# Four VectorE steps of a fused two-layer model's first layer, moved to ScalarE and to accumulating DMAs

## The chip, the core and the metric

The kernel runs on one NeuronCore of a Trainium2 chip. Five engines work side by side, each with its own instruction queue that is worked through in order: PE (TensorE, matrix products; its weight loads are shown apart as PEld), DVE (VectorE), ACT (ScalarE), POOL (GpSimd) and SP (SyncE, which only starts DMAs here). ACT and POOL can start DMAs too. The metric is the device time of one launch in microseconds (us). The kernel before took 2626.24 us, the median of 3 runs (2625.56 to 2628.49).

## The reference: what is computed

Two layers, each `x + attention(norm(x)) + experts(norm(x))`, for 8 samples of 512 tokens with 256 features, all in float32. Only the attention of layer 0 is touched. For one sample, with `xn` the normalised input:

```python
xc  = conv(xn, conv_w)                 # 3 taps along the tokens, each feature by itself
dx  = xc - xn
xxx = xn + dx * maa_x                  # the first mixed input
t5  = tanh(xxx @ maa_w1)               # from it, five mixing weights w, k, v, r, g
m   = einsum(t5, maa_w2)
xw, xk, xv, xr, xg = xn + dx * (maa_w + m[0]), ...
r, k, v = xr @ Wr, xk @ Wk, xv @ Wv ;  g = silu(xg @ Wg)
w   = time_decay + tanh(xw @ decay_w1) @ decay_w2
y   = forward scan + backward scan of S = exp(-exp(w)) * S + k v, read with r
y   = y * sigmoid(dx @ gate_w + gate_b)
yn  = groupnorm(y) * ln_w + ln_b       # the norm and its affine
x   = x + yn * g @ Wo + experts(xn)    # the residual
```

The experts of layer 0 choose 2 of 8 per token; layer 1 has two attentions (one full, one in a window of 64) and 16 small experts.

## The kernel before

Features lie on the 128 partitions in two halves (`c` = 0, 1), tokens along the free axis; so most steps come as two instructions on 128x512 tiles. `big` and `mix` allocate tiles of both halves, 128x1024.

**Order of the work.** Everything in layer 0 is written as Python generators, and `Turns.turn()` advances each of them to its next `yield` once per turn. What the generators issue in this order is the order of the queues of PE, DVE, ACT and SP (`PINNED`); POOL is not pinned, its order is chosen by the planner of the language. A `yield` between an instruction and its user thus sets how many turns of other work lie between them; it starts nothing by itself. In the scan stage one step of the scans is four turns.

**Stages of layer 0.** The prologue normalises the 8 samples (`norm_and_route`, which also writes `xn` transposed to DRAM as `lines[b]` and scores the experts) and runs `projections(0)` beside it; in this stretch each of its three generators is put into the list of a turn twice, so it advances two yields per turn. The scans begin only when `projections(0)` has set `("scans", 0)`. Then `scans` runs, for each sample, 16 steps of four DVE instructions on 128x1024 (lines 942, 951, 959, 964). Beside it, in the same turns, run the placement of the tokens, the 39 chunks of expert matmuls (`experts`), `projections(b + 1)` while sample b is scanned, and `ending(b, c)`, which is added after the last step of each half. `ending(b, 0)` so runs from the middle of sample b's steps on, `ending(b, 1)` in the first turns of sample b + 1; the last one, `ending(7, 1)`, runs after the scans, in the tail.

**`projections`** has three generators. `inputs` loads `xnT` (line 782, SP), makes `dx` in place (789 the first scale, 791 the two taps), then `xxx` (798), then the t5 matmuls on PE (808) and their tanh on ACT (815). `values` and `decays` wait for `inputs`; they contain `mixed`, in which DVE forms `dx * (maa + m)` from PSUM (770), POOL starts a DMA that adds `xn` to it from `xnT` (774, `accum_op=ALU.add`), and after 4 turns (3 for sample 0) PE reads the sum. `xxx` and all other mixed inputs share a pool of two tiles (`xf`). `xnT` has one buffer.

**`ending`**: y times the sigmoid (991), centering by a matmul (995), square (998), variance by matmuls (1006), square root and reciprocal (1012, 1014), spread and transposed (1017, 1023), then DVE's multiply by the inverse deviation (1026), DVE's affine with `ln_w` and `ln_b` (1027) and POOL's multiply by `g` (1028). After the second half, two rounds of eight output matmuls into the one bank of `ps_e` (1038), each followed by DVE's residual add from PSUM into `x` (1043). `x` was loaded by SP when c was 0 (987), and SP stores it to `after[b]` two turns after the last add (1046). SP's queue also carries all loads of `kv` for the scans (916), 8 for each step, into four buffers.

**Into layer 1.** Its tiles take the memory of layer 0's, and its first ACT and DVE instructions (1186, 1188) come after the last store of `x` from it.

Of the kernel before, what the change touches and what calls it, by code (L numbers as in the profile page):

```python
# [28 lines left out]
AF = mybir.ActivationFunctionType  # L29
ALU = mybir.AluOpType  # L30
# [7 lines left out]
B, T, D = 8, 512, 256  # L38
NC = D // P
# [3 lines left out]
PAD = 2  # L43
# [86 lines left out]
def bc(ap, axis, n):  # L130

    shape = list(ap.shape)
    shape.insert(axis, n)
    return ap.unsqueeze(axis).to_broadcast(shape)


def tokens(x):
    return x.rearrange("(n p) d -> p n d", p=P)
# [33 lines left out]
def two_layers(ctx: ExitStack, tc: tile.TileContext, a: dict, out: bass.AP):  # L172
    nc = tc.nc
    vec_e, act_e, pool_e, pe = nc.vector, nc.scalar, nc.gpsimd, nc.tensor
# [33 lines left out]
    def V(name, c):  # L208
        return vecs[:, VEC[name], c : c + 1]
# [177 lines left out]
    with ExitStack() as l0:  # L387
# [302 lines left out]
        def projections(b):  # L690


            first = b == 0
            made[b] = {}

            def big(tag, bufs=2):
                return rw.tile([P, NC, T], F32, tag=tag, name=f"{tag}_{b}", bufs=bufs)

            def bank(name):
                return ps_rw.tile([P, T], F32, tag="rw", name=f"{name}_{b}")  # L700
# [5 lines left out]
            def mix(name, i, other=False):  # L706

                if other and first:
                    return held(i, [P, NC, T], f"{name}_{b}")
                return rw.tile([P, NC, T], F32, tag="xf", name=f"{name}_{b}", bufs=2)  # L710
# [32 lines left out]
            xnT = rw.tile([P, NC, T + 2 * PAD], F32, tag="xnT", name=f"xnT_{b}")  # L743
            xT = [xnT[:, c, PAD : PAD + T] for c in range(NC)]
            dx = big("dx", 1)
            dxs = [dx[:, c, :] for c in range(NC)]
# [4 lines left out]
            def shifted(c, s):  # L751
                return xnT[:, c, PAD + s : PAD + s + T]
# [26 lines left out]
            def inputs():  # L779
                pool_e.memset(xnT[:, :, 0:PAD], 0.0)  # L780
                pool_e.memset(xnT[:, :, PAD + T :], 0.0)
                nc.sync.dma_start(
                    xnT[:, :, PAD : PAD + T], lines[b].rearrange("(c p) t -> p c t", p=P)
                )
                for _ in range(3):
                    yield
                for c in range(NC):
                    o = dx[:, c, :]
                    vec_e.tensor_scalar(o, xT[c], V("conv1", c), None, ALU.mult)
                    for s, n in ((-1, "conv0"), (1, "conv2")):  # L790
                        vec_e.scalar_tensor_tensor(o, shifted(c, s), V(n, c), o, ALU.mult, ALU.add)
                    yield
                for _ in range(0 if first else 1):
                    yield
                both = mix("xxx", 0)
                xxx = [both[:, c, :] for c in range(NC)]
                for c in range(NC):
                    vec_e.scalar_tensor_tensor(
                        xxx[c], dxs[c], V("maa_x", c), xT[c], ALU.mult, ALU.add
                    )  # L800
                for _ in range(1 if first else 2):
                    yield
                both = ((t5a, 0, 0, P), (t5b, P, 64, 96))
                pss = []
                for _, lo, r0, r1 in both:
                    ps = bank(f"t5{lo}")
                    for c in range(NC):
                        pe.matmul(
                            ps[r0:r1, :], m1w[:, c, lo : lo + r1 - r0], xxx[c],
                            start=c == 0, stop=c == NC - 1,  # L810
                        )
                    pss.append(ps)
                    yield
                for (t5, _, r0, r1), ps in zip(both, pss):
                    act_e.activation(t5, ps[r0:r1, :], AF.Tanh)
                yield
                done.add(("inputs", b))
# [21 lines left out]
            def decays():  # L839
# [66 lines left out]
                made[b]["g"] = g  # L906

            return inputs(), values(), decays()


# [16 lines left out]
        def scans(turns):  # L927
# [4 lines left out]
            for n, (b, c, vg) in enumerate(todo):  # L932
# [33 lines left out]
                def sums(b=b, c=c, vg=vg, kv=kv, y=y, z=z, x=x):  # L966
                    for i in range(NV):

                        r0, at = (vg * NV + i) % 4 * 32, (vg * NV + i) // 4
                        pe.matmul(  # L970
                            y[r0 : r0 + 32, :], C["take"][:, 24 - 8 * at : 56 - 8 * at],
                            kv[:, i, :], start=at == 0, stop=at == 3, skip_group_check=True,
                        )
                    if vg == STEPS - 1:
                        turns.add(ending(b, c, y, z, x))
# [7 lines left out]
        def ending(b, c, y, z, x):  # L983

            sig, g = made[b]["sig"], made[b]["g"]
            if c == 0:
                nc.sync.dma_start(x, tokens(a["x"][b]))


            yg = rw.tile([P, T], F32, tag="gn", name=f"yg{c}_{b}", bufs=2)  # L990
            vec_e.tensor_tensor(yg, sig[:, c, :], y, ALU.mult)
            yield
            yield
            yc = ps_e.tile([P, T], F32, tag="e", name=f"yc{c}_{b}")
            pe.matmul(yc, C["center"], yg, start=True, stop=True)
            yield
            sq = rw.tile([P, T], F32, tag="gn", name=f"sq{c}_{b}", bufs=2)
            act_e.activation(sq, yc, AF.Square)
            zc = z[:, c, :]
            act_e.copy(zc, yc)  # L1000
            yield
            yield

            var = ps_rw.tile([P, NT, 8], F32, tag="rw", name=f"var{c}_{b}")
            for t in range(NT):
                pe.matmul(
                    var[:, t, :], sq[:, t * P : (t + 1) * P], C["mean"][:, :8],
                    start=True, stop=True,
                )
            yield  # L1010
            sd = rw.tile([P, NT, 8], F32, tag="sd", name=f"sd{c}_{b}")
            act_e.activation(sd, var, AF.Sqrt, bias=geps)
            yield
            vec_e.reciprocal(sd, sd)
            yield
            wide = rw.tile([P, NT, HD, 8], F32, tag="gn", name=f"wide{c}_{b}", bufs=2)
            act_e.copy(wide, bc(sd, 2, HD))
            yield
            yield
            rs = ps_rw.tile([P, T], F32, tag="rw", name=f"rs{c}_{b}")  # L1020
            for t in range(NT):
                cols = slice(t * P, (t + 1) * P)
                pe.transpose(rs[:, cols], wide[:, t, :, :].rearrange("p v h -> p (v h)"), ident)
            yield
            yield
            vec_e.tensor_tensor(zc, zc, rs, ALU.mult)
            vec_e.tensor_scalar(zc, zc, V("ln_w", c), V("ln_b", c), ALU.mult, ALU.add)
            pool_e.tensor_tensor(zc, zc, g[:, c, :], ALU.mult)
            yield
            if c + 1 < NC:  # L1030
                return
            made.pop(b)
            yield
            for t in range(0, NT, 2):
                ps = ps_e.tile([P, 2, D], F32, tag="e", name=f"o{t}_{b}")
                for i in range(2):
                    for k in range(NC):
                        pe.matmul(
                            ps[:, i, :], z[:, k, (t + i) * P : (t + i + 1) * P], wmix[:, 4, k, :],
                            start=k == 0, stop=k == NC - 1,  # L1040
                        )
                yield
                vec_e.tensor_tensor(x[:, t : t + 2, :], x[:, t : t + 2, :], ps, ALU.add)
            yield
            yield
            nc.sync.dma_start(tokens(after[b]), x)

        for b in range(B):
# [562 lines left out]
```

## Time and profile before

| | |
|---|---|
| Median of 3 runs | 2626.24 us |
| Profiled execution, its own time | 2629.75 us |
| Its span (first to last instruction) | 2628.0 us |
| Mean granted TensorE clock | 0.931 |
| ACT busy | 934.0 us, 36% |
| POOL busy | 475.5 us, 18% |
| DMA, moved in all | 269.80 MB, mean 103 GB/s |
| First step of the scans starts | 99.1 us |
| Last scan instruction of layer 0 ends | about 1394 us |
| First instructions of layer 1 | about 1438 us |

The page gives busy times over the whole span, which has stages with different limits, so the views by stretch count for more than the shares. "Idle before" and "waited for" tell what ended an engine's idle time, by the semaphores; a short wait can hide behind another. In a group's line, "x14 | 9.7, 737 | 0.0" is 14 instructions, 9.7 us together, 737 ns each in the mean, and no idle time before them.

### The profile page before, as it was taken

To read this page: it belongs to the slowest core of one execution; us is meant where nothing else is said; L and a number is where in the kernel's file an instruction comes from. 1 tells how busy PE (TensorE), PEld (TensorE's weight loads), DVE (VectorE), ACT (ScalarE), POOL (GpSimd) and SP (SyncE) were. 2 spreads that over 40 slices of the span, in tenths; PEclk is the share of its full clock that TensorE was granted. 3 is DMA by queue.
4 is the path that set the end of the run, shared out by engine and by line. 5 is a ranking of instruction groups with operands and counts; after the bars stand their busy time and mean duration, and the time that the engine had idled before them with its cause. 6 is when DMAs were issued, how large, how long until landed. Compare 5 with 4: busy or idle time off the path is not lost. (4 is left out here: it accounts for less than half of the span.)

```text
span 2628.0 us, 32310 instructions
## 1 busy us (share of the span) xinstructions
PE 2318.2 (88%) x11772; PEld 1373.0 (52%) x11772; DVE 2064.8 (79%) x2759; ACT 934.0 (36%) x1731; POOL 475.5 (18%) x408
## 2 busy tenths in 40 slices
PE   6599988889989888999845799999999999999998
PEld 4265555555655555655622445554555555555555
DVE  7799989789899987999986655676767668685566
ACT  1334241242322423223101244444444444445444
POOL 1123232323223322332221110010101010000000
PEclk9789998989989989999965899999999999999999
DMA  6646675556657556665552100010110101000000
GB/s 221 162 110 172 174 204 148 153 149 180 193 162 205 152 147 186 175 169 166 154 155 81 57 25 25 9 45 29 33 33 25 37 21 41 17 21 21 21 1 25
DMA packets 111708, 269.80 MB, mean 103 GB/s; under 512 B 25632, under 2 KB 51008, under 8 KB 106432
## 3 DMA queue, kind: packets, MB, share of 16 engines
q0 software_dynamic: 32048, 136.73, 18.7%
q1 hardware_dynamic: 70528, 113.32, 15.7%
q10 hardware_dynamic: 8976, 17.70, 1.9%
q8 instruction: 95, 1.56, 0.2%
q14 instruction: 61, 0.50, 0.1%
HBM read 215.22 MB, written 31.46 MB: 94 GB/s over the span
## 5 line engine op out<-in xcount | busy, mean ns | idle before, releaser
L670 PE MATMUL y<-wdn,h 128*128 128x256 f32 x936 | 274.8, 431 | 43.8 <-DVE h L639 41.4
L951 DVE TENSOR_TENSOR_SCAN kv<-dqs,kv 128x1024 f32<-128x1024 f32 x128 | 292.0, 2282 | 3.1
L959 DVE TENSOR_TENSOR_SCAN kv<-ds,kv 128x1024 f32<-128x1024 f32 x128 | 292.7, 2287 | 1.6
L670 PEld LDWEIGHTS y<-wdn,h 128*128 128x128 f32 x936 | 177.4, 206 | 163.8 <-issue 86.4
L630 PE MATMUL g<-xsT,wgu 128*128 128x256 f32 x936 | 230.4, 390 | 0.7 <-ACT xsT L616 0.7
L1330 ACT ACTIVATE pt_g<-sc_g 128x512 f32<-128x512 f32 (+1 forms) x384 | 170.9, 532 | 151.3 <-PE sc_g L1322 143.5
L1480 PE MATMUL y<-w,h 128*128 128x256 f32 x768 | 203.5, 403 | 5.6 <-DVE h L1469 4.8
L630 PEld LDWEIGHTS g<-xsT,wgu 128*128 128x128 f32 x936 | 177.3, 194 | 53.8 <-issue 30.7
L1424 PE MATMUL g<-xT,w 128*128 128x512 f32 x384 | 193.8, 627 | 9.7 <-DVE h L1466 4.4
L630 PE MATMUL u<-xsT,wgu 128*128 128x256 f32 x780 | 195.4, 390 | 0.2
L1424 PE MATMUL u<-xT,w 128*128 128x512 f32 x384 | 191.4, 621 | 1.8 <-DVE h L1466 0.9
L630 PEld LDWEIGHTS u<-xsT,wgu 128*128 128x128 f32 x780 | 146.9, 193 | 56.0 <-issue 23.9
L1480 PEld LDWEIGHTS y<-w,h 128*128 128x128 f32 x768 | 139.2, 194 | 62.7 <-issue 35.9
L964 DVE TENSOR_TENSOR kv<-kv,r 128x1024 f32<-128x1024 f32 x128 | 164.5, 1285 | 3.4
L942 DVE TENSOR_TENSOR kv<-kv,k 128x1024 f32<-128x1024 f32 x128 | 155.9, 1218 | 13.3 <-DMA w<-in_w 8.2
L654 ACT ACTIVATE h<-g 128x512 f32<-128x512 f32 (+1 forms) x117 | 61.4, 526 | 277.1 <-PE g L630 252.0
L1330 ACT ACTIVATE pt_l<-sc_l 128x384 f32<-128x384 f32 (+1 forms) x256 | 98.2, 471 | 122.6 <-PE sc_l L1322 82.4
L970 PE MATMUL ys<-kv,cst 128*32 128x512 f32 x512 | 96.3, 668 | 50.9 <-DVE kv L964 50.9
L592 POOL DMA_INDIRECT xs<-normed,whose x78 | 121.3, 1555 | 79.2 <-DVE whose L576 47.3
L1467 DVE TENSOR_TENSOR h<-h,u 128x512 f32<-128x512 f32 x96 | 66.1, 688 | 78.3 <-PE u L1424 74.1
L1338 DVE TENSOR_TENSOR pt_l<-pt_l,cst 128x768 f32<-128x768 f32 (+1 forms) x128 | 108.0, 885 | 17.9 <-ACT pt_l L1330 17.9
L1338 DVE TENSOR_TENSOR pt_g<-pt_g,cst 128x512 f32<-128x512 f32 x128 | 85.1, 686 | 39.1 <-ACT pt_g L1330 38.9
(311 smaller groups left out, 3795.0 us busy)
## 6 DMA issues: line engine op xcount, KB each, us to landing
kv<-vd SPq DMA_DIRECT2D x1024, 64.0 KB
xf<-xnT POOLq DMA_DIRECT2D x40, 512.0 KB, 6.6
cb<-cd SPq DMA_DIRECT2D x128, 128.0 KB
outs<-ys POOLq DMA_DIRECT2D x39, 256.0 KB, 6.3
w<-in_w ACTq DMA_DIRECT2D x12, 384.0 KB
xn<-in_x SPq DMA_DIRECT2D x8, 512.0 KB
xnT<-xT ACTq DMA_DIRECT2D x16, 256.0 KB
normed<-xn SPq DMA_DIRECT2D x8, 512.0 KB
```

Of the source, the lines that this page charges most:

```text
L592: pool_e.indirect_dma_start(out=xs[:, n, :], out_offset=None, in_=normed, in_offset=bass.IndirectOffsetOnAxis(ap=whose[:, at : at + 1], ax ...
L630: pe.matmul(o, w[:, at + c * P : at + (c + 1) * P], xT[:, c, :], start=c == 0, stop=c == NC - 1,)
L670: pe.matmul(y[:, n, :], hs[j // 2][lo:, j % 2, n * P : (n + 1) * P], wd[lo:, j * D : (j + 1) * D], start=j == 0, stop=j == NJ0,)
L942: vec_e.tensor_tensor(kv, kv, bc(kc, 1, NV), ALU.mult)
L951: vec_e.tensor_tensor_scan(out=flat, data0=qc, data1=flat, initial=0.0, op0=ALU.mult, op1=ALU.add)
L959: vec_e.tensor_tensor_scan(out=flat[:, ::-1], data0=dc[:, ::-1], data1=flat[:, ::-1], initial=0.0, op0=ALU.mult, op1=ALU.add,)
L964: vec_e.tensor_tensor(kv, kv, bc(rc, 1, NV), ALU.mult)
L970: pe.matmul(y[r0 : r0 + 32, :], C["take"][:, 24 - 8 * at : 56 - 8 * at], kv[:, i, :], start=at == 0, stop=at == 3, skip_group_check=True,)
L1330: act_e.activation(pt[:, i, :end], scs[i][:, :end], AF.Exp, scale=0.25)
L1338: vec_e.tensor_tensor(pt[:, :, a0 : a0 + m], pt[:, :, a0 : a0 + m], bc(mask[:, :m], 1, 4), ALU.mult,)
L1424: pe.matmul(ps, w[:, k, c * P : (c + 1) * P], xT[:, c, :], start=c == 0, stop=c == NC - 1,)
L1480: pe.matmul(y[:, i, :], hs[k][:, (t + i) * P : (t + i + 1) * P], w1[j - 5 + k][:, 2, :], start=k == 0, stop=k == 5,)
```

## The change

- **dx's first scale.** DVE's multiply of `xn` by `conv1` becomes an ACT multiply for both halves, one turn ahead of DVE's two taps. `inputs` is one turn longer by it.
- **The first mixed input.** DVE's `dx * maa_x + xn` becomes an ACT multiply `dx * maa_x` and one DMA from POOL's queue that adds `xn` out of `xnT`; the t5 matmuls follow 4 turns later (3 for sample 0), in place of 2 (1).
- **The norm's affine.** DVE's multiply and add with `ln_w` and `ln_b` becomes one ACT instruction (Identity with a per-partition scale and bias), one turn after DVE's multiply and one turn ahead of POOL's.
- **The residual.** SP's load of `x` goes. ACT copies the two output banks into `x`, a DMA from POOL's queue adds the layer's input from DRAM to it, and SP's store is issued 8 turns after that DMA.

```diff
@@ inputs
                 for _ in range(3):
                     yield
                 for c in range(NC):
+                    act_e.mul(dx[:, c, :], xT[c], V("conv1", c))
+                yield
+                for c in range(NC):
                     o = dx[:, c, :]
-                    vec_e.tensor_scalar(o, xT[c], V("conv1", c), None, ALU.mult)
                     for s, n in ((-1, "conv0"), (1, "conv2")):
                         vec_e.scalar_tensor_tensor(o, shifted(c, s), V(n, c), o, ALU.mult, ALU.add)
                     yield
...
                 for c in range(NC):
-                    vec_e.scalar_tensor_tensor(
-                        xxx[c], dxs[c], V("maa_x", c), xT[c], ALU.mult, ALU.add
-                    )
-                for _ in range(1 if first else 2):
+                    act_e.mul(xxx[c], dxs[c], V("maa_x", c))
+                pool_e.dma_start(both, xnT[:, :, PAD : PAD + T], accum_op=ALU.add)
+                for _ in range(3 if first else 4):
                     yield
@@ ending
             sig, g = made[b]["sig"], made[b]["g"]
-            if c == 0:
-                nc.sync.dma_start(x, tokens(a["x"][b]))
...
             vec_e.tensor_tensor(zc, zc, rs, ALU.mult)
-            vec_e.tensor_scalar(zc, zc, V("ln_w", c), V("ln_b", c), ALU.mult, ALU.add)
+            yield
+            act_e.activation(zc, zc, AF.Identity, bias=V("ln_b", c), scale=V("ln_w", c))
+            yield
             pool_e.tensor_tensor(zc, zc, g[:, c, :], ALU.mult)
...
                 yield
-                vec_e.tensor_tensor(x[:, t : t + 2, :], x[:, t : t + 2, :], ps, ALU.add)
-            yield
-            yield
+                act_e.copy(x[:, t : t + 2, :], ps)
+            pool_e.dma_start(x, tokens(a["x"][b]), accum_op=ALU.add)
+            for _ in range(8):
+                yield
             nc.sync.dma_start(tokens(after[b]), x)
```

## The prediction

> **What bounds the kernel now.** I read the page, then the busy times by stretch, the waits of PE and DVE, the costliest groups, and the timeline of both ends of layer 0. The page's busy line:
>
> ```profile
> PE 2318.2 (88%) x11772; PEld 1373.0 (52%) x11772; DVE 2064.8 (79%) x2759; ACT 934.0 (36%) x1731; POOL 475.5 (18%) x408
> ```
>
> No engine is the bound throughout. The chain on the page covers only the last 5% of the span (from 2501 us), so for layer 0 I go by stretches: 0 to 99 us is the prologue, 99 to 1397 the scans beside the experts, 1397 to 1438 the tail, then layer 1 with PE at 95%. A sample's scans are 16 steps; I cut them into quarters of four steps (16 turns) at VectorE's first instruction of a step. First quarters of samples 1, 2 and 3, and the second one of sample 3; the columns are the stretch, its length, then busy us (and instructions) of PE, PEld, DVE, ACT, POOL, the granted clock, the DMA share, GB/s:
>
> ```profile
> 278.60:318.90 40.30, 38.11 (x151) 22.67 (x150) 39.21 (x37) 13.98 (x20) 13.98 (x9) 0.93 0.47 150
> ...
> 433.90:482.90 49.00, 39.28 (x145) 23.94 (x146) 40.47 (x39) 14.75 (x21) 9.66 (x7) 0.90 0.43 117
> ...
> 610.20:650.60 40.40, 35.34 (x131) 21.01 (x128) 39.78 (x39) 11.31 (x17) 11.09 (x9) 0.95 0.55 160
> 650.60:692.00 41.40, 41.40 (x161) 26.93 (x159) 33.80 (x28) 7.75 (x13) 13.80 (x11) 0.93 0.73 181
> ```
>
> DVE fills 97 to 98% of the first quarters of samples 1 and 3, but PE has only 2.2 and 5.1 us to spare there. Sample 2's is lock-step: both engines wait, 8 to 10 us each. In second quarters PE is full. The pattern repeats every three samples (4 as 1, 5 as 2, 6 as 3). So a microsecond taken off DVE is worth at most what PE has idle in that quarter. Waits of the scan stage (us, times, longest), PE first, then DVE:
>
> ```profile
> PE t L808 <- DVE xxx L798: 9.9, 4, 3.6
> PE v L729 <- DMA xf<-xnT: 6.1, 3, 2.7
> ```
> ```profile
> DVE xf L770 <- PE m L764: 30.5, 15, 5.7
> ...
> DVE dq L884 <- ACT near L879: 9.4, 7, 2.0
> ```
>
> **The change, part by part.** Removed from DVE within the scan stage, with one ACT row to price the replacement:
>
> ```profile
> L1027 DVE TENSOR_SCALAR z<-z,vecs 128x512 f32<-128x512 f32 x15 | 9.7, 650 | 0.5
> L798 DVE SCALAR_TENSOR_TENSOR xxx<-dx,vecs,xnT 128x512 f32<-128x512 f32 x14 | 9.7, 737 | 0.0
> ...
> L1043 DVE TENSOR_TENSOR x<-x,o 128x512 f32<-128x512 f32 x14 | 9.6, 688 | 10.8 <-PE o L1038 10.6
> ...
> L789 DVE TENSOR_SCALAR dx<-xnT,vecs 128x512 f32<-128x512 f32 x14 | 7.1, 507 | 0.0
> ```
> ```profile
> L861 ACT ACTIVATE d<-w,vecs 128x512 f32<-128x512 f32 x14 | 9.1, 686 | 0.3
> ```
>
> Relief: 9.7 + 9.7 + 9.6 + 7.1 = 36.1 us of DVE, 4.5 us of it in a full first quarter (dx 1.0, xxx 1.5, affine 0.65, residual 1.38), 0.65 in a third quarter (the affine of c = 0). What it is worth, quarter by quarter: sample 0 has inputs only, PE idle 24 us: 2.4. Samples 1 and 4: PE's 2.2 idle each, 4.4. Samples 3 and 6: PE idle 5.1 and 5.8 against 4.5 removed, I take 4 each, 8. Sample 7 has the ending only: 2.0. Samples 2 and 5, lock-step: half of 4.5 each, 4.4. Third quarters: seven at half of 0.65, one in full, 3. Sum 24 us. Bounds: 10 (lock-step everywhere) and 36 (all of it).
>
> Added on ACT: 57 instructions of 0.58 us (plain copies) to 0.69 us (L861, with a per-partition operand), some 37 us. Cover: ACT is busy 28 to 35% of a first quarter. If that cover were gone, the work would simply have changed engines and the relief of 24 be nothing. The Trainium skill speaks against the move (ScalarE: Activation LUTs, Rules for kernel authors: plain multiplies and adds belong on VectorE): by its formula (What ACT_TABLE_LOAD costs) an instruction with one such operand takes 280 + 0.833 x 512 = 707 ns, close to L861, against 507 and 650 on DVE. As a rule for time on the path it would leave the other terms below alone, +25.5; by the rows ACT is off the path and the relief stands. No row shows Identity; the same page (Table sets) says that it is in every set, and the trace has loads at no Copy line. Were there two loads each time, 16 x 2 x 1.28 us (L654's load) is 41 us on ACT, still under its idle time.
>
> Waits added. (1) DVE's first dx instruction (L791) waits for ACT's two multiplies, issued one turn (some 2.5 us) ahead, and the scan instructions are queued behind it. Nearest row: dq waiting for near, 9.4/7 = 1.3 us each, with a longer ACT chain. Bounds 0 and 1.3; I take 0.4, in 7 samples 3 us. (2) PE's t5 matmuls (L808) wait for the accumulate into xxx, with projections and expert matmuls queued behind. ACT's multiplies are issued in turn 7, PE in turn 11: 10 us. Needed: ACT 1.3, POOL's issue 1.34, landing 6.6, together 9.2. The same kind of DMA today:
>
> ```profile
> L774 POOL DMA_DIRECT2D xf<-xnT x40: 1183/1340/1810, 61.5 to 1220.6; - x40
> ...
> DMA to landing us min/median/max: 5.1/6.6/9.8
> ```
>
> xf has the same four turns, and PE waits for it 10 us in all over 21 mixes, up to 4.2 us in one quarter. For xf PE is held to DVE by the matmul just before; for xxx nothing holds it, and today it already runs ahead into xxx (9.9 us). Bounds 0 and 4 each; I take 1.3, in 7 samples 9 us. That is on top of the old wait, which is spent in the relief. (3) POOL gets 16 accumulates (8 xxx, 8 x) of 1.3 us and waits in its queue for ACT; behind it are the weight and row loads, which land 6 to 9 us after issue for a use more than 10 later, and no PE wait on them is shown today: nothing. (4) SP loses x's load (0.42 us) and stores x eight turns (20 us) after the accumulate instead of two turns after DVE's add. Accumulate and issue take 8 to 10 us of the 20, so SP's kv loads behind the store come no later: nothing; were the landing over 20 us, they would starve the next scan. (5) The affine adds two turns ahead of POOL's multiply; the output matmul stays two turns behind it: nothing. (6) DMA: 8 x 512 KB more on 269.8 MB, at 60% share: nothing.
>
> The ends have no cover. Prologue:
>
> ```profile
> 39.86 6.57 PE L808 MATMUL t<-xxx,m1w 128*128 128x512 f32 x8 [5.67 <-DVE xxx L798]
> ...
> 52.18 1.94 PE L764 MATMUL m<-t5a,m2a 32*128 32x512 f32 x4
> ```
>
> PE waits for xxx even now, and all of projections(0) follows. In place of xxx (39 to 40.5 us) the second dx pair falls there, then ACT 1.3, POOL 1.3 and 6.6 to land: 49 to 50. Then the 6.6 us of t5, score and transpose matmuls of the next norms (4 us), copies and tanh on ACT (2.5): the first m at 62 in place of 52. Of those 10 us some 4 come back, since one turn of norm work (score and transposes, expert choice) now lies ahead of the chain: +6, bounds 2 and 10. Tail:
>
> ```profile
> 1432.37 0.69 DVE L1043 TENSOR_TENSOR x<-x,o 128x512 f32<-128x512 f32 x1 [3.59 <-PE o L1038]
> ...
> 1433.09 0.38 SPq L1046 DMA_DIRECT2D after<-x  x1
> ...
> 1437.92 0.88 DVE L1188 TENSOR_SCALAR xg_g<-xT,vecs 128x512 f32<-128x512 f32 x2 [4.86 <-DMA after<-x]
> ```
>
> Layer 1's first work waits for the last store of x. Between add and store comes POOL's accumulate: 6.6 us from issue to landing, plus 0.9 for its wake-up and for an affine that ACT may run behind the copy of cT: +7.5, bounds 5 and 10; PE is full from 1500 on and gives none back. Here the skill would say less: DMA: Bandwidth & Descriptors (Anatomy of one DMA) fits 2.0 us + bytes/436 GB/s, 3.2 us for 512 KB, a tail of about +4 and a sum 3.4 lower. The row is 6.6 and I take it.
>
> Sum: -24 + 3 + 9 + 6 + 7.5 = +1.5 us. It stands against the profiled execution (2629.75 us, its span 2628.0), which is 3.5 us over the median of the runs, 2626.24; I add it to the median: **2628**.
>
> **Rivals.** *Slower: the xxx accumulate lands late.* Place: L808 in the first quarters of samples 1 to 7. For it: PE's lead over DVE there, and an issue-to-landing time of up to 9.8. Against: the four turns nearly cover 9.2. At 4 us each (the xf wait of samples 2 and 5) it costs 28 in place of 9: +20, 2646. It decides above 1.8 us a sample. *Faster: the relief counts almost in full.* For it: DVE at 97% in five of seven first quarters, and PE's wait for xxx there goes. Against: PE has 2 to 5 us to give. With 30 of 36 us, no new wait and ends of 13.5: -16, 2610. *The relief moves nothing:* PE sets each quarter, DVE only waits more. For it: lock-step in samples 2 and 5, PE full in second quarters; against: DVE without a wait in the others. Left are the ends and the new waits at half: 2626 + 13.5 + 6 = 2646, or 2640 without waits; I put 2642.
>
> **How the numbers follow.** Forecast 0.45 (its own range 2619 to 2638), late accumulate 0.25, full relief 0.22, no relief 0.08. About 0.2% (5.3 us) is what a measurement of this kernel can tell: the band is 2621 to 2631.5. Faster: 0.21 of the full relief and 0.06 of the forecast, 0.27. Same: 0.24, nearly all the forecast's. Slower: 0.15 of the forecast, 0.25, 0.08 and rounding, 0.49. The range takes in the centres of the rivals and the nearer part of the bounds: 2607 to 2651; beyond lie 36 us of relief with no wait, and 28 + 9 us of waits with the long ends.
>
> **What would show it.** DVE's busy time down 41 us, ACT's up about as much, with no new table loads; a wait of t (L808 before) for DMA xxx near 1 to 2 us a sample; first quarters 1 to 4 us shorter; scans starting some 6 us later; layer 1's first instruction 7 to 8 us behind the end of the tail's copy work. The prediction is wrong if kv loads or expert weights make an engine wait, if POOL's queue puts an accumulate behind a load that waits for PE, or if first quarters keep their length.

## The result, and the profile after

The changed kernel takes 2659.45 us, the median of 4 runs (2657.73 to 2664.2). The kernel before, run beside it on the same chip, takes 2625.9 (2625.36 to 2628.49). The ratio is 1.0129, 95% interval 1.0111 to 1.0146: **slower by 1.3%, some 34 us**, where 2628 was forecast with a range up to 2651.

The busy times moved the way that was forecast. The page's line for the changed kernel:

```profile
PE 2333.0 (88%) x11772; PEld 1384.7 (52%) x11772; DVE 2027.7 (76%) x2695; ACT 976.6 (37%) x1795; POOL 497.5 (19%) x424
```

DVE has 37.1 us less (41 was forecast), ACT 42.6 more (about 41), POOL 22 more. DVE became freer and the kernel slower, so the page's shares do not hold the answer; the stretches do. I cut both traces at the same events; each column is one profiled execution. "Scan stage" runs from DVE's first multiply of kv by k to 7 us behind the start of the last one, "tail" from there to layer 1's first DVE instruction; the four sums are the quarters of all 8 samples (4 steps each).

| us | before | after | difference |
|---|---|---|---|
| First step of the scans starts | 99.1 | 113.8 | +14.7 |
| Scan stage | 1294.6 | 1306.7 | +12.1 |
| of it first quarters | 360.4 | 316.1 | -44.3 |
| second quarters | 313.2 | 347.0 | +33.8 |
| third quarters | 377.2 | 380.9 | +3.7 |
| fourth quarters | 243.8 | 262.7 | +18.9 |
| Tail | 44.2 | 49.9 | +5.7 |
| Layer 1 | 1190.1 | 1187.8 | -2.3 |
| Span | 2628.0 | 2658.2 | +30.2 |

The first quarters gained more than the 36.1 us that was taken off DVE, and second and fourth quarters lost more than that. These are sample 1's second quarter before the change, then first and second quarters of samples 1, 2 and 3 after it (samples are counted from 0; the columns are stretch, length, busy us and instructions of PE, PEld, DVE, ACT, POOL, granted clock, DMA share, GB/s):

```profile
318.90:357.90 39.00, 38.57 (x162) 25.68 (x161) 34.67 (x30) 6.86 (x13) 12.60 (x10) 1.00 0.83 210
```
```profile
298.00:336.40 38.40, 28.29 (x110) 17.47 (x110) 33.59 (x28) 11.42 (x18) 9.71 (x6) 0.91 0.65 168
336.40:386.70 50.30, 49.23 (x190) 31.65 (x190) 36.39 (x33) 14.90 (x23) 16.48 (x13) 0.97 0.65 171
472.40:508.00 35.60, 29.05 (x126) 18.72 (x125) 34.98 (x29) 12.72 (x20) 7.12 (x6) 1.00 0.76 197
508.00:552.10 44.10, 43.26 (x171) 27.13 (x171) 35.82 (x32) 11.86 (x19) 17.00 (x14) 1.00 0.77 207
632.50:668.10 35.60, 32.24 (x130) 20.44 (x127) 35.13 (x30) 13.89 (x21) 12.13 (x9) 1.00 0.73 195
668.10:710.20 42.10, 39.84 (x154) 25.05 (x154) 34.79 (x30) 8.63 (x16) 13.74 (x12) 0.97 0.77 200
```

Look at the instruction counts of PE. In sample 1's first quarter PE had 151 matmuls and has 110; the second had 162 and has 190. Sample 2's move the same way (145 to 126, and 145 to 171), sample 3's hardly. So the quarters of samples 1 and 2 do not hold the same work any more: the next sample's projections come later, in sample 1 PE stands idle for 10 us of the first quarter, and the second takes 50.3 us in place of 39.0. The waits from 99 to 1450 us (us, times, longest) name what is late there; PE first, then DVE:

```profile
PE g L729 <- DMA xf<-xnT: 24.3, 8, 6.3
PE t L809 <- DMA xxx<-xnT: 13.0, 2, 6.8
```
```profile
DVE kv L943 <- DMA kv<-vd: 41.5, 9, 8.3
DVE h L639 <- PE u L630: 35.9, 19, 6.7
DVE q L871 <- ACT d L863: 23.2, 8, 8.9
DVE sd L1013 <- ACT sd L1011: 21.1, 7, 3.7
```

Before, the same lines were 3.9 (g), 2.7 (kv), 13.0 (h), 0.6 (q) and 5.5 (sd). Only the wait of t is for something that the change put in. The others are of parts that it leaves as they were.

**The ends.** The prologue of the changed kernel, in the timeline:

```profile
39.33 1.45 POOL L801 DMA_DIRECT2D xxx<-xnT  x1 [3.58 <-ACT xxx L800]
46.80 6.31 PE L809 MATMUL t<-xxx,m1w 128*128 128x512 f32 x8 [5.88 <-issue]
...
58.20 1.52 PE L764 MATMUL m<-t5a,m2a 32*128 32x512 f32 x4 [2.28 <-ACT t5a L816]
```

The first m matmul is at 58.20 in place of 52.18, +6.0. The other 8.7 us come between it and the scans. And the tail, where from the accumulate's issue to the store of x there are 7.5 us:

```profile
1459.80 1.43 POOL L1045 DMA_DIRECT2D x<-in_x  x1 [6.21 <-ACT x L1044]
1467.30 0.38 SPq L1048 DMA_DIRECT2D after<-x  x1
...
1470.45 0.88 DVE L1190 TENSOR_SCALAR xg_g<-xT,vecs 128x512 f32<-128x512 f32 x2 [20.52 <-DMA after<-x]
```

### The profile page after: what moved, and what is told of

It is laid out like the page before. It is cut to its first block, busy times and chain, and to the rows that moved or that the text cites. A ratio compares the mean times of both kernels' runs of the same rounds, so it can differ in the third digit from the quotient of the medians.

```text
span 2658.2 us, 32351 instructions
## 1 busy us (share of the span) xinstructions
PE 2333.0 (88%) x11772; PEld 1384.7 (52%) x11772; DVE 2027.7 (76%) x2695; ACT 976.6 (37%) x1795; POOL 497.5 (19%) x424
## 5 line engine op out<-in xcount | busy, mean ns | idle before, releaser
L670 PE MATMUL y<-wdn,h 128*128 128x256 f32 x936 | 268.7, 423 | 34.9 <-DVE h L639 31.9
L943 DVE TENSOR_TENSOR kv<-kv,k 128x1024 f32<-128x1024 f32 x128 | 156.0, 1219 | 48.4 <-DMA kv<-vd 41.5
L971 PE MATMUL ys<-kv,cst 128*32 128x512 f32 x512 | 105.2, 679 | 58.7 <-DVE kv L965 58.6
L654 ACT ACTIVATE h<-g 128x512 f32<-128x512 f32 (+1 forms) x117 | 61.4, 526 | 238.2 <-PE g L630 224.9
L582 POOL DMA_INDIRECT wgu<-in_w_gu,wrow x39 | 68.6, 1759 | 303.1 <-PE u L630 301.1
```

The source lines that it names most:

```text
L670: pe.matmul(y[:, n, :], hs[j // 2][lo:, j % 2, n * P : (n + 1) * P], wd[lo:, j * D : (j + 1) * D], start=j == 0, stop=j == NJ0,)
L943: vec_e.tensor_tensor(kv, kv, bc(kc, 1, NV), ALU.mult)
L971: pe.matmul(y[r0 : r0 + 32, :], C["take"][:, 24 - 8 * at : 56 - 8 * at], kv[:, i, :], start=at == 0, stop=at == 3, skip_group_check=True,)
```

## The experiments

Two theories came from these traces. *Shifted turns*: three turns added to `inputs` move the whole chain of the next sample's projections against everything else that is written turn by turn. *Queues*: what was added to POOL's and SP's queues holds up the kv loads and the accumulates into xf.

### One part at a time

Each kernel is the kernel before with one of the four parts of the change, its turns included.

```diff
# e1: the dx part
+                    act_e.mul(dx[:, c, :], xT[c], V("conv1", c))
+                yield
-                    vec_e.tensor_scalar(o, xT[c], V("conv1", c), None, ALU.mult)
# e2: the xxx part
-                    vec_e.scalar_tensor_tensor(xxx[c], dxs[c], V("maa_x", c), xT[c], ALU.mult, ALU.add)
-                for _ in range(1 if first else 2):
+                    act_e.mul(xxx[c], dxs[c], V("maa_x", c))
+                pool_e.dma_start(both, xnT[:, :, PAD : PAD + T], accum_op=ALU.add)
+                for _ in range(3 if first else 4):
# e3: the affine part; e4: the residual part, both as in the change
```

> The kernel before with one part of the change alone: the first scale of dx goes to ACT, one turn ahead. Theory 'shifted turns' (each turn added to the inputs pushes the next sample's projections out of the first quarter, where PE has gaps, into the second, where it has none): prologue +3 us, the scan stage some 3 us longer in spite of 7.1 us less work on DVE, total +3 to +7 us. Theory 'queues' (the loss comes from kv loads that SP issues late, behind the store of x and the write of vd): prologue +3, scan stage -3 to 0 since nothing is added to SP or POOL; total -1 to +3 us.

> The kernel before with xxx alone moved: ACT's multiply, POOL's accumulate, and the two turns that are added before the t5 matmuls. 'Shifted turns': this is the main part of the loss; prologue +9 us, scan stage +5 to +12 us, with first quarters shorter and second quarters longer; total +14 to +21 us. 'Queues': the prologue's +9 us and a wait of PE for the accumulate; scan stage -5 to +3; total +4 to +12 us.

> The kernel before with the norm's affine alone on ACT, with its two turns. 'Shifted turns': the ending's turns lie behind PE's projections and feed no projection, so the 9.7 us of relief count for something: -6 to 0 us. 'Queues': no DMA is added; likewise -6 to 0 us. If the turns before POOL's multiply delay the output matmul into a full quarter: 0 to +4 us.

> The kernel before with the residual alone moved: ACT copies the matmul's result into x, POOL accumulates the input into x, the store follows eight turns later. Tail +6 us in each theory. 'Shifted turns': the inputs keep their turns, so the scan stage gains 0 to 6 us from 9.6 us of relief; total 0 to +6 us. 'Queues': SP's store, moved to the middle of the second quarter, and POOL's accumulate hold the kv loads up; DVE's wait for kv grows from 3 us to 20 us or more; total +12 to +20 us.

| kernel | ratio to before | 95% interval | in us | scan stage | third quarters |
|---|---|---|---|---|---|
| before | | | | 1294.6 | 377.2 |
| e1, dx | 1.0248 | 1.0228 to 1.0268 | +65 | 1368.8 | 440.0 |
| e2, xxx | 1.0179 | 1.0159 to 1.0200 | +47 | 1340.0 | 373.7 |
| e3, affine | 0.9973 | 0.9963 to 0.9983 | -7 | 1286.7 | 370.4 |
| e4, residual | 1.0034 | 1.0017 to 1.0051 | +9 | 1290.8 | 378.8 |

Both theories missed e1 and e2 by far. The dx part alone, one turn and two ACT instructions a sample, costs nearly twice what the whole change costs, and the four parts add up to +114 us against +34 for all of them together. So no price by part exists, and "first quarters against second quarters" is not the mechanism either: e1 loses most in its third quarters. Nor does the prologue have a price by part: the scans start at 99.9 us in e1 and 98.9 in e2, against 99.1 before, where 3 and 9 us had been expected. The affine gained 7 us, a little over its expectation. The residual alone has its tail (+4.5 us). DVE's wait for kv rises from 2.7 to 21.0 us, but the scan stage is no longer for it, and it is not SP's store that holds these loads up: of the two waits, in samples 2 and 5, the first ends at 513.34 us, and the store is issued at 513.60, behind the loads; ahead of them SP had waited 6.4 and 10.2 us for the next sample's v. The total lies between the two expectations.

### Only the turns

What is left of e1 when its moved work is taken out is one `yield`.

```diff
# e5, on the kernel before
                 for _ in range(3):
                     yield
+                yield
                 for c in range(NC):
                     o = dx[:, c, :]
# e6: the same, and
-                for _ in range(1 if first else 2):
+                for _ in range(3 if first else 4):
```

> The kernel before with nothing moved to another engine: one empty turn is added to the inputs, ahead of the dx work. Theory 'place in the turns': a turn moves the next sample's chain against the ending of the sample in the scans, so PE's dw matmul (which waits for the accumulate into xf) comes to stand ahead of the ys matmuls that DVE's yg instruction waits for. Then this kernel loses what the dx part alone lost, +55 to +75 us, with third quarters at 55 to 60 us in place of 46 to 51. Theory 'moved work' (the loss of the dx part comes from ACT's multiplies and DVE's wait for them): -3 to +6 us.

> The kernel before with nothing moved: the three turns that the change adds to the inputs (one ahead of dx, two ahead of the t5 matmuls), empty. 'Place in the turns': second quarters longer by 2 to 10 us as in the changed kernel, scan stage 15 to 40 us longer, since the relief of DVE is missing; total +18 to +45 us. 'Moved work': the turns only delay the prologue; 0 to +8 us.

With one empty turn: ratio 1.0305 (1.0283 to 1.0328), +80 us, a little more than the 55 to 75 expected; third quarters 437.9. With three: 1.0160 (1.0140 to 1.0181), +42 us. Nothing was moved to another engine in either. **The `yield`s alone cost more than the whole change does**; the moved work gives some of it back. Three waits of e6 from 99 to 1450 us are nearly those of the changed kernel:

```profile
DVE kv L943 <- DMA kv<-vd: 48.5, 13, 9.7
PE g L729 <- DMA xf<-xnT: 23.4, 8, 5.4
DVE sd L1015 <- ACT sd L1013: 21.1, 7, 3.7
```

The waits of h for u (20.1 us) and of q for d (13.2) have grown too, but less than in the changed kernel (35.9 and 23.2). So the late kv loads and the late accumulates into xf are no effect of the added DMAs on POOL and SP, which e6 doesn't have. *Queues*, as a theory of what was added to them, falls as the main cause.

What one turn does is seen around the start of sample 3's third quarter, first in the kernel before, then in e5. A "[...]" is the idle time of the engine just before, and what ended it:

```profile
684.77 2.58 POOL L774 DMA_DIRECT2D xf<-xnT  x2 [2.39 <-DVE xf L770]
...
688.70 3.05 POOL L582 DMA_INDIRECT wdn<-in_w_dn,wrow  x1 [1.35 <-PE y L670]
...
692.00 1.93 PE L847 MATMUL dw<-xf,dw 128*64 128x512 f32 x4
```
```profile
722.20 1.40 DVE L770 SCALAR_TENSOR_TENSOR xf<-m,vecs,dx 128x512 f32<-128x512 f32 x2
...
724.77 1.78 POOL L582 DMA_INDIRECT wdn<-in_w_dn,wrow  x1 [8.02 <-PE y L670]
...
727.31 2.60 POOL L774 DMA_DIRECT2D xf<-xnT  x2
...
736.62 3.64 PE L848 MATMUL dw<-xf,dw 128*64 128x512 f32 x4 [6.74 <-DMA xf<-xnT]
...
740.19 1.20 PE L971 MATMUL ys<-kv,cst 128*32 128x512 f32 x8
...
741.50 0.69 DVE L992 TENSOR_TENSOR yg<-sig,ys 128x512 f32<-128x512 f32 x1 [8.07 <-PE ys L971]
```

Before, POOL issues the two accumulates into xf as soon as DVE has made the first tile, and a gather of expert weights (L582) behind them. In e5 that gather, which waits 8 us for PE's y, stands ahead of them, and they are issued 3.7 us after DVE has finished both tiles. It is so in all seven samples of e5 that follow the first: the first accumulate comes 1.1 to 7.7 us after its tile, 32 us together, behind gathers for the experts that waited for PE; before, it comes after 0.3 us each time. POOL's queue is the one that is not pinned, and one turn in `inputs` was enough to change its order. PE waits at dw for the accumulate, issued 9.3 us ahead. Behind dw in PE's queue stand the ys matmuls, for which DVE's yg waits; and behind yg in DVE's queue stand the scans. One late DMA stops both engines that carry the stage. In the kernel before the same dw starts 7.2 us after its accumulate's issue with no gap, and yg waits 2.5. The waits of yg and dw in e5, 7 samples each:

```profile
DVE yg L992 <- PE ys L971: 50.0, 7, 11.2
PE dw L848 <- DMA xf<-xnT: 48.9, 7, 11.4
DVE sd L1015 <- ACT sd L1013: 43.0, 7, 7.6
```

They were 15.8, 3.6 and 5.5. With three turns instead of one, dw falls behind yg (in the changed kernel 715.0 us for yg, 718.5 for dw in that sample), yg waits 4.2 us in all there (6.0 in e6), the accumulate ahead of dw comes 0.3 us after its tile again, and other neighbours collide.

e10 tests the chain from dw to yg: e5's turn stays, and yg moves two turns down, with the rest of the ending behind it.

```diff
# e10, on e5
+            yield
+            yield
             yg = rw.tile([P, T], F32, tag="gn", name=f"yg{c}_{b}", bufs=2)
```

> The kernel before with the one empty turn in the inputs and two empty turns ahead of the ending's yg instruction. If that one turn costs because DVE's yg waits for ys behind the dw matmul: yg's wait of 50 us in the scan stage falls under 15, third quarters lose 25 to 45 us of their 437.9, total +25 to +55 us against the kernel before. If yg's wait is only where a general shortage of PE shows: the wait goes to another instruction, third quarters stay within 10 us of 437.9, total +68 to +85 us.

Ratio 1.0183 (1.0168 to 1.0198), +48 us: two more empty turns in another place give 32 of the 80 us back. Third quarters 407.7, yg's wait 17.0 (under 15 was expected), while dw's stays at 52.3, as POOL's accumulates stay late. The chain dw, ys, yg is thus a large part of the loss of e5, though not all: DVE's wait of h for u grew to 41 us, and PE has a new wait of 53 us, of rs for DVE's xf. No run puts POOL's order back by itself, so how much of the 80 us is due to it stays open.

e11 goes the other way, with nothing moved: from sample 2 on the next sample's inputs start one turn earlier.

```diff
# e11, on the kernel before; sample 1 is added at the start of sample 0 as before
                 yield
+                if (c, vg) == (NC - 1, STEPS - 1) and b + 2 < B:
+                    turns.add(then(*projections(b + 2)))
                 vec_e.tensor_tensor(kv, kv, bc(rc, 1, NV), ALU.mult)
```

> The kernel before with nothing moved, the next sample's inputs starting one turn earlier from sample 2 on. If the place of the kernel before is only good against the turns behind it, one turn the other way is harmless: -8 to +6 us. If its place is a narrow optimum: +15 to +60 us.

Ratio 1.0105 (1.0089 to 1.0122), +28 us. Of the places tried, that of the kernel before is a narrow optimum: one turn down costs 80 us, three 42, one up 28. So a start that is merely earlier is no gain.

### The place given back

If the place is the cause, the changed kernel is mended by starting the chain as much earlier as it got longer.

```diff
# e7, on the changed kernel; sample 1 is added at the start of sample 0 as before
                 if n + 1 == len(todo):
                     done.add(("spread",))
                 yield
+                if (c, vg) == (NC - 1, STEPS - 1) and b + 2 < B:
+                    turns.add(then(*projections(b + 2)))
```

> The changed kernel, with the next sample's inputs started three turns earlier, from sample 2 on, so that its t5 matmuls and all behind them keep the turns that they had before the change. 'Place in the turns': quarters of samples 1 to 6 return to the lengths before, less the relief; scan stage 10 to 30 us shorter than in the changed kernel's 1306.8; total -4 to +14 us against the kernel before. 'Moved work': the scan stage stays near 1307; total +28 to +36 us.

Ratio 0.9986 (0.9971 to 1.0001). The changed kernel's loss of 34 us is gone, with 4 us to spare, and no ACT instruction, no DMA and no turn was taken out of it. The scan stage is 1274.8, which is 32 us under the changed kernel and **20 us under the kernel before**. First and second quarters of samples 1 and 3:

```profile
301.10:337.80 36.70, 36.09 (x144) 22.21 (x143) 36.27 (x32) 15.81 (x23) 15.15 (x11) 1.00 0.72 193
337.80:379.70 41.90, 40.05 (x167) 26.12 (x165) 33.70 (x29) 8.61 (x16) 15.72 (x11) 1.00 0.88 211
626.20:666.00 39.80, 36.14 (x135) 21.68 (x132) 37.61 (x34) 13.31 (x20) 12.49 (x9) 0.91 0.60 174
666.00:703.60 37.60, 37.55 (x156) 24.82 (x156) 32.72 (x27) 8.90 (x15) 16.85 (x12) 1.00 0.89 209
```

PE's 144 and 167 matmuls in sample 1 are near the 151 and 162 of before: the work is back in its quarters. And PE hardly waits for the new accumulate:

```profile
PE t L809 <- DMA xxx<-xnT: 0.7, 2, 0.3
```

### The ends

```diff
# e8, on the changed kernel: the first sample's dx and xxx, and the last sample's
# residual, in the form of before; for example
+                    if first:
+                        vec_e.scalar_tensor_tensor(xxx[c], dxs[c], V("maa_x", c), xT[c], ALU.mult, ALU.add)
+                    else:
                         act_e.mul(xxx[c], dxs[c], V("maa_x", c))
+                if not first:
                     pool_e.dma_start(both, xnT[:, :, PAD : PAD + T], accum_op=ALU.add)
...
+                if last_b:
+                    vec_e.tensor_tensor(x[:, t : t + 2, :], x[:, t : t + 2, :], ps, ALU.add)
+                else:
                     act_e.copy(x[:, t : t + 2, :], ps)
# e9: e8 and e7 together
# e12, on e9
-                act_e.dma_start(vd.rearrange("(c p) t -> p c t", p=P), v)
+                pool_e.dma_start(vd.rearrange("(c p) t -> p c t", p=P), v)
```

> The changed kernel, with the first sample's dx and xxx and the last sample's residual in the old form (VectorE, no accumulate, no added turns), all else as changed. By the two traces the prologue gives back 14.7 us and the tail 5.8: total +10 to +16 us against the kernel before. By the forecast's terms (6 and 7.5): +16 to +22 us. If the ends shift what follows them in the turns as well, a value outside both.

> The two mends together: the changed kernel with the next sample's inputs started three turns earlier from sample 2 on, and with the first sample's dx and xxx and the last sample's residual in the old form. If the place in the turns and the ends are separate terms, their gains add: scan stage near 1275 us, prologue near 100, tail near 44, total -20 to -30 us against the kernel before. If the ends' gain comes back as lower clock or later waits: -3 to -10 us.

> The kernel with both mends, and the write of v to memory issued by POOL in place of ACT. If SP's kv loads are held by their wait for ACT's write of the next sample's v: DVE's wait for kv falls from 30 to 35 us of the scan stage to under 12, and the scan stage is 10 to 20 us shorter than that of the kernel with both mends alone. If the kv loads are late for another reason (SP issues them late, or transfers are slow), the wait stays, and the total is within 4 us of that kernel.

| kernel | ratio to before | 95% interval | scans start | scan stage | tail |
|---|---|---|---|---|---|
| after | 1.0129 | 1.0111 to 1.0146 | 113.8 | 1306.7 | 49.9 |
| e8, ends as before | 1.0041 | 1.0024 to 1.0058 | 100.9 | 1304.4 | 43.4 |
| e7, place as before | 0.9986 | 0.9971 to 1.0001 | 117.1 | 1274.8 | 48.7 |
| e9, both | 0.9924 | 0.9910 to 0.9939 | 102.9 | 1273.8 | 44.6 |
| e12, both, and v written by POOL | 0.9865 | 0.9850 to 0.9881 | 98.6 | 1261.0 | 44.0 |

The stages are those of one profiled execution each; that of e7 took 2630.81 us, 9 more than the median of its runs, which its late prologue may hold a part of. The ends cost 23 us (after less e8) or 16 (e7 less e9), by the traces 20.4; the place costs 38 (after less e7) or 31 (e8 less e9). The two are separate terms to within 7 us. What is then left of the change, in e9, is a gain of 20 us by the ratio: 2606.0 us, the median of 6 runs, against 2623.57 of the kernel before beside it (18 by the medians).

e12 follows a wait that is left in e9. SP issues the kv loads of the running sample, and in its queue it waits for ACT's write of the *next* sample's v. In the waits of e9 (first SP over the span, then DVE in the scan stage):

```profile
SPq L927 <- DMA vd<-v: 118.6, 8, 29.1
```
```profile
DVE kv L953 <- DMA kv<-vd: 32.6, 5, 8.7
```

The longest of the eight, 29.1 us, is sample 0's own v in the prologue. The other seven, 89.5 us in all and 10 to 16 each, fall in the sixth or seventh of a sample's 16 steps and are for the next sample's v. With that write on POOL's queue, in e12, only the one of the prologue is left:

```profile
SPq L927 <- DMA vd<-v: 27.0, 1, 27.0
```
```profile
DVE kv L953 <- DMA kv<-vd: 6.3, 3, 3.0
```

The scan stage falls by 12.8 us as expected, the scans start 4.3 us earlier, and the kernel takes 2590.37 us (4 runs, 2584.82 to 2591.0), 1.35% under the kernel before. The two buffers of v in DRAM give these loads no reason to wait for the next sample's v; why SP's queue does so the trace doesn't say, and it stays open. The kernel before has the same seven waits, shorter (55.9 us, 10.3 at most), and there DVE waits only 2.7 us for kv; e12's edit was not tried on it.

## Why the prediction was wrong

**The step that failed.** The sum held each quarter's work fixed: "a microsecond taken off DVE is worth at most what PE has idle in that quarter". The added turns entered it only as cover for the accumulate ("ACT's multiplies are issued in turn 7, PE in turn 11") and, in the affine, as "nothing". That all of `values` and `decays` hangs behind `inputs` and would come three turns later had no term. In its place the runs show that this shift costs 31 to 38 us (after against e7, e8 against e9), or +42 us when the turns come alone (e6). The instruction counts of PE by quarter, which the forecast's own table had, are where it shows first. The whole is then the sum of what e7, e8 and e9 take apart: the place +31 to +38, the ends some +20, the moved work -20.

**Relief, -24, and the two new waits, +3 and +9.** With the place kept, the scan stage gained 19.8 us (e7) and 20.8 (e9), against a net -12. The relief of 24 was about right, the two waits too high. In e7 PE waits for the accumulate into xxx 0.7 us in all, where 9 was taken, and no wait of DVE for ACT's dx stands in the scan stage's list. In the changed kernel as it is, PE waited 13.0 us for xxx, but only in samples 1 and 4 (6.8 at most). One reading under this sum was too broad: "in second quarters PE is full" holds for samples 1 and 3, while in sample 2's PE is busy for 38.60 of 45.20 us.

**POOL's and SP's queues, "nothing".** Right of what was added, and wrong of the order. Two signs that the prediction had named against itself did come: kv loads that make DVE wait (41.5 us), and accumulates that POOL's queue puts behind a load that waits for PE. The longest waits of g, 6.0 and 6.3 us in samples 1 and 4, follow accumulates that POOL issued 5.3 us after their tile, behind the gather of L582; in e6 it is 3.0 us in the same places, and in e5 the sign is at its largest. Both come from the turns, with no DMA added.

**Prologue, +6, bounds 2 to 10.** The first m matmul came 6.0 us later, the number that was worked out, though the t5 matmuls ahead of it began at 46.80 us and not at 49 to 50. But the scans came 14.7 later. Between the first m and the scans, before and after:

```profile
52.18:99.10 46.92, 41.33 (x135) 19.71 (x134) 29.08 (x66) 21.34 (x30) 6.48 (x6) 0.83 0.52 135
```
```profile
58.20:113.80 55.60, 50.14 (x126) 24.86 (x126) 22.17 (x43) 20.84 (x29) 5.03 (x5) 0.69 0.40 98
```

PE is idle for 5.5 us in both, and busy for 41.33 us at a granted clock of 0.83 before and 50.14 us at 0.69 after; the products, 34.3 and 34.6, are nearly the same. The term lacked the clock.

**Tail, +7.5, bounds 5 to 10.** It measured 5.7 (4.5 in e4 and e7). From the accumulate's issue to SP's store there are 7.5 us, so the row of 6.6 us was the right one to take.

**ACT.** Busy 42.6 us more against 41 forecast; in the list of groups the table loads at L654 went from 25 to 27, and none stands at the moved lines. The affine takes longer than the 0.69 us of its row, with two per-partition operands:

```profile
L1027 ACT ACTIVATE z<-z,vecs 128x512 f32<-128x512 f32 x16 | 13.0, 814 | 32.9 <-DVE z L1025 32.4 <-ACT cT L380 0.4
L788 ACT ACTIVATE dx<-xnT,vecs 128x512 f32<-128x512 f32 x16 | 10.7, 714 | 5.0 <-DMA xnT<-xnT 4.5 <-ACT xT L438 0.5
```

ACT was off the path, as the prediction took it to be, against the Trainium skill's rule that puts plain multiplies and adds on VectorE (ScalarE: Activation LUTs, Rules for kernel authors): e3 moves the affine alone and gains 7 us.

**The rivals.** None was this one. "The xxx accumulate lands late" gave the nearest time (2646) through a wait that is 0.7 us once the place is right.

## What to carry to other kernels

Where the order of the queues is written out by hand, an edit that lengthens one chain by a turn is two edits: what it moves, and where everything behind it now falls against the other chains; test the second alone, with empty turns, before pricing the first. Count each engine's instructions by stretch before and after: if the counts move between stretches, savings by stretch can't simply be added up. Look at the order of the queue that isn't pinned as well. When an edit needs more turns, start its chain that much earlier, and keep the first and the last round, which have no cover, in the old form.

## What was not expected of the hardware

The loss of clock in the prologue has a form. In both traces the granted clock is 1.00 or 0.50 there, in stretches of about 3.4 us or multiples of it. In the changed kernel:

```profile
58.80:69.00 10.20, 10.20 (x33) 6.83 (x30) 2.70 (x6) 0.59 (x1) 0.00 (x0) 0.50 0.15 51
75.90:92.90 17.00, 17.00 (x44) 9.41 (x45) 6.12 (x16) 2.35 (x4) 2.43 (x2) 0.50 0.61 121
```

Up to the scans' start the changed kernel spends about 34 us at half clock, the kernel before about 16 (52.4 to 59.2, 69.4 to 72.8, 93.3 on). The difference, 18 us at half speed, comes to an estimated 9 us, close to the 8.7 that the prologue lost beyond the first m. The Trainium skill (TensorE: Matmul & The Clock Gate, What's actually happening) has these two states and windows of about 3.4 us, and puts the half clock down to an idle window. The first stretch follows a gap of PE of 2.3 us, the 5.9 us of idle time ahead of the t5 matmuls (for which the view names no releaser; the accumulate into xxx was under way) being 12 us back. The second has no gap of PE over 1.5 us anywhere between 58.2 and 99.6 us, and PE is shown busy throughout; so the rule agrees in form here, and what set the second stretch off stays open. e7, with the same prologue, repeats it (half clock from 58.6 to 68.8 and from 72.2 to 96.1, scans at 117.1); with the old form the scans start at 98.6 to 102.9. e6, with the old instructions and three empty turns, has a mean of 0.85 as well: its first m comes at 52.06 us, no later than before, but it spends 31 us at half clock and starts its scans at 105.8. So about half of what the prologue lost comes with the turns alone. Half clock is not paid in full everywhere: e10 spends 6.5 us at it, 9.5 less than the kernel before, and starts its scans at the same 99.0.
